# Router products of the residual as eight extra channels of the offset convolution, added behind PSUM, in a fused deformable-convolution, attention and mixture-of-experts kernel

## The chip, the cores and the metric

The kernel runs on one core of a Trainium2 chip, in one launch. The metric is the device time of that launch in microseconds. Everything is float32.

## The reference, cut to what matters

Four images of 256 channels and 64 x 64 pixels go through one layer of three parts. The change lies in the first part, and in a product that the third part needs.

```python
B, C, H, W = 4, 256, 64, 64
# 1: deformable 3x3 convolution of the group-normalized image, with a residual
n = groupnorm(x, groups=32)
om = conv3x3(n, w_off) + b_off            # 27 channels: 9 taps x (dy, dx), 9 masks
sampled[k] = bilinear(n, y + ky + dy[k], x + kx + dx[k]) * sigmoid(mask[k])
x = x + sum_k w_conv[:, :, k] @ sampled[k]
# 2: attention over the 4 images, on layer-normalized tokens
t = tokens(x)                             # 4 x 4096 tokens of 256
t = t + attention(layernorm(t))
# 3: mixture of 8 experts, each token to the best two
u = layernorm(t)
logits = u @ router_w.T                   # 8 columns
t = t + u + sum over the best two of gate_e * (gelu(u @ w1[e] + b1[e]) @ w2[e] + b2[e])
```

The router's product is linear up to the layer norm. So the kernel carries `t @ router_w.T`, eight columns, beside the 256 columns of `t` from the convolution on. A row of the convolution's output has `CR = 264` columns: 256 channels, and the eight products of those channels with the router's weights.

## The kernel before, in words

The first stage is the convolution, and it takes the first 2124 us. A prologue prepares image 0. Then come 1152 steps (`STEPS = 288` for each image): one step is one tap `k` of the nine for one tile `r` of 128 pixels. Nine steps make a tile, four tiles make a group of 512 pixels, whose output goes to DRAM in one store. The steps are written out by hand: within `tc.manual_schedule` the program order is each engine's order. For step `n`:

- `gather(n + 10)` and `gather(n + 11)`, for even `n`, are indirect DMAs that POOL issues (L577): for each of 128 pixels the four corners of the bilinear sample, 4 KB a pixel, from a `table` in DRAM, into one of ten buffers `g`. The first of the two waits for the last corner that reads the buffer.
- `corner0(n + 3)` on ACT (L593) starts the weighted sum `s` of the corners; `corners(n + 2)` on DVE (L601) adds the others, three operations a step, each with the gathered corner and `s` as inputs, both in SBUF.
- `turned(n)` on PE (L615) transposes `s` into PSUM, `to_sbuf(n)` on ACT (L621) copies it to `sT`.
- `product(n - 1)` on PE (L640) multiplies `sT` with the weights of the tap, 264 columns, and adds up in `acc`, a PSUM buffer for the tile. At the first tap of a tile it also adds the residual: two transposes of `xraw` (L628) give the 256 columns, and two products of `xraw` with the router's weights `rwc_sb` (L634) give the eight.
- `done`, once a tile, on ACT (L649): it copies the 264 columns of the tile that ended one step earlier from PSUM into `outs`, which has two buffers for groups of four tiles. After the fourth tile SP issues the store (L651).

In between, `pieces(b + 1)` prepares the next image, at due steps from step 32 on: group statistics on DVE (L302), the group norm's scale `rs` and shift `nb`, and from step 56 on eight `block`s, one every 22 steps. A block normalizes ten rows into `xs` on ACT (L362), transposes eight of them into the table (L369, L378, four stores on SP, L384), and runs the offset convolution: six PE products `po` of three taps by 32 channels, 96 rows (L396), three shifted copies of 32 rows each on ACT into `oc` (L408), four products with `tap_sum` that sum the three taps and transpose to pixels (L417), and a copy `kept` on DVE into `om` (L426). After the last block `positions` on DVE makes indices and weights. Image 3 has no next image, so there are no blocks beside its steps. Image 0's first three offset blocks and its whole table are made in the prologue, its other five offset blocks beside its own steps. In the prologue the tile framework orders the instructions, not the program by hand; its weights come by DMAs on SP, in the order `xraw`, `woff_sb` (L232), `boff_sb`, `wconv_sb` (L250), `rwc_sb`, and the router's columns of `wconv_sb` are made by `routed` at its end.

The two later stages, attention with the router's choice and the experts, read the stored rows and are not touched. In them L942 on DVE mixes the values of the images, with one input in PSUM and one in SBUF, L990 on DVE adds eight router columns in PSUM to such columns in SBUF, and L1105 is POOL's scatter of tokens.

Of the kernel before, what the change touches and what calls it, by code (L numbers as in the profile page):

```python
# [9 lines left out]
F32 = mybir.dt.float32  # L10
# [7 lines left out]
P = 128  # L18
# [52 lines left out]
def conv_attn_moe_kernel(  # L71
# [127 lines left out]
    with ExitStack() as actx:  # L199
# [26 lines left out]
        load_image(0)  # L226


        woff_sb = aw.tile([P, NCH, 3, 3, QUAD], F32, name="woff_sb")
        V.memset(woff_sb, 0.0)  # L230
        for ch in range(NCH):
            nc.sync.dma_start(  # L232
                woff_sb[:, ch, :, :, :NOFF],
                w_off[ch * P : (ch + 1) * P].rearrange("p (ki kj) o -> p ki kj o", kj=3),
            )
        boff_sb = aw.tile([3 * QUAD, 1], F32, name="boff_sb")
        V.memset(boff_sb, 0.0)
        nc.sync.dma_start(boff_sb[QUAD : QUAD + NOFF], b_off.unsqueeze(1))
        tap_sum = aw.tile([3 * QUAD, NOFF], F32, name="tap_sum")
        for kj in range(3):  # L240
            ps = slice(kj * QUAD, (kj + 1) * QUAD)
            V.tensor_copy(tap_sum[ps], ident[ps, kj * QUAD : kj * QUAD + NOFF])


        ocs = [aw.tile([3 * QUAD, RB, W], F32, name=f"oc{n}") for n in range(3)]
        for oc in ocs:
            V.memset(oc, 0.0)
        wconv_sb = aw.tile([P, NCH, K2, CR], F32, name="wconv_sb")
# [34 lines left out]


        params, stores = {}, {}

        def pieces(b):

# [8 lines left out]
            ve = asm.tile([P, NCH], F32, name=f"ve{b}", tag="gve", bufs=2)  # L297
            rs = asm.tile([P, NCH], F32, name=f"rs{b}", tag="grs", bufs=2)
            pm = []

            def stats(ch, j):
                V.bn_stats(st[:, ch, j, :], xr[:, ch, j * BLK : (j + 1) * BLK])  # L302
# [27 lines left out]
                (n + 5, lambda: G.tensor_tensor(rs, ve, nhalf[:, :NCH], ALU.pow))  # L330
            )
            out_.append((n + 7, shift))
            n += 8

            xrv = xr.rearrange("p ch (h w) -> p ch h w", w=W)
# [3 lines left out]
            def block(q, at, table=True, offsets=True, alone=False):  # L339

                out_ = [] if alone else later
                y0 = q * RB - 1
                lo, hi = max(y0, 0), min(y0 + RB + 2, H)
                t = {}
                between = "" if table else "_"

                def norm(ch):
                    if ch == 0:
                        t["xs"] = apad.tile(
                            [P, NCH, RB + 2, W], F32, name=f"xs{b}_{q}{between}",  # L350
                            tag=f"xs{between}", bufs=2 if table else 1,
                        )
                        if lo > y0:
                            G.memset(t["xs"][:, :, 0, :], 0.0)
                        if hi < y0 + RB + 2:
                            G.memset(t["xs"][:, :, RB + 1, :], 0.0)
                    to, of = t["xs"][:, ch, lo - y0 : hi - y0], xrv[:, ch, lo:hi]
                    scale, bias = rs[:, ch : ch + 1], nb[:, ch : ch + 1]
                    if alone:
                        V.tensor_scalar(to, of, scale, bias, ALU.mult, ALU.add)  # L360
                    else:
                        S.activation(to, of, AF.Identity, bias=bias, scale=scale)  # L362


                def turn(i):
                    xc = t["xs"][:, :, 1 : RB + 1].rearrange("p ch y x -> p ch (y x)")
                    t["tp"] = ps_tp.tile([P, C], F32, name=f"tpx{b}_{q}_{i}", tag="tp")
                    for ch in range(NCH):
                        T.transpose(  # L369
                            t["tp"][:, ch * P : (ch + 1) * P], xc[:, ch, i * P : (i + 1) * P],  # L370
                            ident,
                        )

                def leave(i):
                    if i == 0:
                        t["zt"] = ast.tile([P, NT, C], F32, name=f"zt{b}_{q}", tag="zt")
                    zt = t["zt"]
                    S.copy(zt[:, i, :], t["tp"])  # L378
                    if i < NT - 1:
                        return  # L380
                    for yl in range(2):
                        for two in range(2):
                            yy = q * RB + yl + 1 - two
                            stores[b] = nc.sync.dma_start(  # L384
                                tv[yy : yy + RB - 1 : 2, 1 : W + 1, two, :].rearrange(
                                    "t x c -> x t c"
                                ),
                                zt[yl * W : (yl + 1) * W],
                            )


                def rows_of(n):
                    if n == 0:
                        t["po"] = ps_om.tile([3 * QUAD, RB, W], F32, name=f"po{b}_{q}", tag="om")
                    ch, ki = divmod(n, 3)
                    T.matmul(  # L396
                        t["po"], woff_sb[:, ch, ki].rearrange("p kj o -> p (kj o)"),
                        t["xs"][:, ch, ki : ki + RB],
                        start=(n == 0), stop=(n == NCH * 3 - 1),
                    )  # L400

                oc = ocs[q % 2 if table else 2]

                def shifted(kj):
                    ps = slice(kj * QUAD, (kj + 1) * QUAD)
                    to = slice(max(0, 1 - kj), W - max(0, kj - 1))
                    of = slice(max(0, kj - 1), W - max(0, 1 - kj))
                    S.activation(  # L408
                        oc[ps, :, to], t["po"][ps, :, of], AF.Identity, bias=boff_sb[ps]
                    )  # L410

                def summed(half):
                    if half == 0:
                        t["pt"] = ps_om.tile([P, NT, NOFF], F32, name=f"pt{b}_{q}", tag="om")
                    ocf = oc.rearrange("p y x -> p (y x)")
                    for i in range(half * 2, half * 2 + 2):
                        T.matmul(  # L417
                            t["pt"][:, i, :], ocf[:, i * P : (i + 1) * P], tap_sum,
                            start=True, stop=True,
                        )  # L420

                def kept():
                    of[q] = om[:, rows_in(q), :] if b else atmp.tile(
                        [P, NT, NOFF], F32, name=f"om{b}_{q}", tag="om_", bufs=2
                    )
                    V.tensor_copy(of[q], t["pt"])  # L426

                out_.append((at, lambda: norm(0)))
                out_.append((at + 1, lambda: norm(1)))
                if table:  # L430
                    for i in range(NT):
                        out_.append((at + 3 + 4 * i, lambda i=i: turn(i)))
                        out_.append((at + 4 + 4 * i, lambda i=i: leave(i)))
                if offsets:
                    for m in range(NCH * 3):
                        out_.append((at + 4 + 2 * m + m // 2, lambda m=m: rows_of(m)))
                    for kj in range(3):
                        out_.append((at + 18 + kj, lambda kj=kj: shifted(kj)))
                    out_.append((at + 22, lambda: summed(0)))
                    out_.append((at + 23, lambda: summed(1)))  # L440
                    out_.append((at + 24, kept))
                return out_
# [180 lines left out]
        def product(n):  # L623
            b, r, k = split(n)
            if k == 0:
                accs[n // K2] = ps_acc.tile([P, BLK], F32, name=f"acc{b}_{r}", tag="acc")
                for ch in range(NCH):
                    T.matmul(  # L628
                        accs[n // K2][:, ch * P : (ch + 1) * P],
                        xraw[b][:, ch, r * P : (r + 1) * P], ident,  # L630
                        start=(ch == 0), stop=False, is_transpose=True,
                    )
                for ch in range(NCH):
                    T.matmul(  # L634
                        accs[n // K2][:, C:CR], xraw[b][:, ch, r * P : (r + 1) * P],
                        rwc_sb[:, ch, :], start=False, stop=False,
                    )
            sT = sTs.pop(n)
            for ch in range(NCH):
                T.matmul(  # L640
                    accs[n // K2][:, :CR], sT[:, ch * P : (ch + 1) * P], wconv_sb[:, ch, k, :],
                    start=False, stop=(k == K2 - 1 and ch == NCH - 1),
                )

        def done(tile_):
            b, r = divmod(tile_, NR)
            if r % NT == 0:
                outs[b] = ast.tile([P, NT, CR], F32, name=f"o{b}_{r}", tag="o")
            S.copy(outs[b][:, r % NT, :], accs.pop(tile_)[:, :CR])  # L649
            if r % NT == NT - 1:  # L650
                nc.sync.dma_start(t1[b][r // NT], outs[b])  # L651

# [902 lines left out]
```

## Time and profile before

| | |
|---|---|
| median of 14 runs | 3582.44 us (3573.46 to 3593.73) |
| profiled execution | 3575.61 us, span of its core 3573.8 us |
| mean granted TensorE clock | 0.929 of full speed |
| busy in the span: PE, DVE, POOL, ACT | 86%, 73%, 56%, 48% |
| HBM traffic | 899 MB, 252 GB/s over the span |
| first stage | steps from 90 us to 2124 us, about 1.77 us each |

In the profile a line names the source line, the engine, the operation and the tiles, output first, `out<-in`. PE is the matmul, PEld the load of the stationary operand, which overlaps it. A number in square brackets in the timeline is the engine's idle time ahead of the operation, with what ended it. The profiled execution is one run; its time stands beside the median in the table.

### The profile page before, as it was taken

How to read it: one execution, taken by the hardware profiler on the slowest of the kernel's cores; microseconds unless marked ns; L12 is line 12 of the kernel's file. 1: busy time of each engine (PE TensorE's matmuls, PEld its weight loads, DVE VectorE, ACT ScalarE, POOL GpSimd, SP SyncE). 2: the span in 40 equal slices, each digit the busy share in tenths (PEclk: the TensorE clock that was granted, in tenths of full speed). 3: DMA queues.
4: the chain of work that ended last, by engine and by line, in shares of the span. 5: the costliest groups of instructions: out<-in, count | busy, mean ns of one | idle time of the engine just before them, and what ended most of it. 6: DMA issues, size and time to landing. Idle time of an engine off the chain costs nothing. (4 is left out here: it accounts for less than half of the span.)

```text
span 3573.8 us, 49706 instructions
## 1 busy us (share of the span) xinstructions
PE 3059.5 (86%) x13658; PEld 2240.1 (63%) x13658; DVE 2605.5 (73%) x6747; ACT 1716.0 (48%) x3913; POOL 2004.8 (56%) x1801
## 2 busy tenths in 40 slices
PE   6799997889988899978777879997888888999995
PEld 4667765667766676756565654443444467888883
DVE  3777786867777777777676768887888864557777
ACT  2456653456544465644444434343333244555652
POOL 1565666766676666677776751110766656554441
PEclk7899998999999999999898889998999999999995
DMA  7899998899999899988788862112544344547778
GB/s 232 326 328 342 337 340 329 286 335 359 342 328 354 304 352 351 345 307 308 281 322 306 294 232 67 55 49 85 179 158 148 102 127 131 164 124 244 240 240 307
DMA packets 322442, 898.89 MB, mean 252 GB/s; under 512 B 43218, under 2 KB 89949, under 8 KB 320120
## 3 DMA queue, kind: packets, MB, share of 16 engines
q0 software_dynamic: 191808, 671.74, 51.8%
q1 hardware_dynamic: 130360, 223.98, 19.6%
q8 instruction: 113, 1.85, 0.2%
q14 instruction: 161, 1.32, 0.1%
HBM read 744.43 MB, written 154.79 MB: 252 GB/s over the span
## 5 line engine op out<-in xcount | busy, mean ns | idle before, releaser
L601 DVE SCALAR_TENSOR_TENSOR s<-g,wts,s 128x256 f32<-128x256 f32 x3456 | 1436.2, 481 | 519.3 <-ACT s L593 354.2
L577 POOL DMA_INDIRECT g<-table,idx x1152 | 1373.4, 1192 | 672.1 <-DVE s L601 393.6
L640 PE MATMUL acc<-wconv_sb,sT 128*128 128x264 f32 x4608 | 1334.7, 415 | 266.0 <-ACT sT L621 166.7
L640 PEld LDWEIGHTS acc<-wconv_sb,sT 128*128 128x128 f32 x4608 | 834.3, 202 | 409.0 <-ACT sT L621 196.0
L621 ACT COPY sT<-tps 128x256 f32<-128x256 f32 x1152 | 424.2, 368 | 736.0 <-PE tps L615 483.4
L593 ACT ACTIVATE s<-g,wts 128x256 f32<-128x256 f32 x1152 | 588.9, 511 | 234.7 <-DMA g<-table,idx 197.2
L615 PEld LDWEIGHTS tps<-ident,s 128*128 128x128 f32 x2304 | 329.1, 149 | 253.1 <-issue 161.6
L615 PE MATMUL tps<-ident,s 128*128 128x128 f32 x2304 | 461.8, 283 | 27.6 <-DVE s L601 23.4
L1379 POOL DMA_INDIRECT ys_rows<-y,to x284 | 282.0, 993 | 293.3 <-DVE y L1376 227.6
L1105 POOL DMA_INDIRECT xs_rows<-u,slots x256 | 259.9, 1015 | 126.9 <-issue 113.2
L1350 PE MATMUL ph<-xT,w 128*128 128x256 f32 x1136 | 276.8, 387 | 21.9 <-ACT hT L1354 11.9
L1368 PE MATMUL py<-w,hT 128*128 128x256 f32 x1136 | 272.8, 384 | 0.0
L1354 ACT ACTIVATE hT<-ph,w 128x256 f32<-128x256 f32 x284 | 133.3, 473 | 233.9 <-PE ph L1350 153.7
L1373 DVE TENSOR_TENSOR y<-py,w 128x512 f32<-128x512 f32 x142 | 98.3, 692 | 200.3 <-ACT w L1312 80.1
L1368 PEld LDWEIGHTS py<-w,hT 128*128 128x128 f32 x1136 | 219.5, 193 | 31.2
L1350 PEld LDWEIGHTS ph<-xT,w 128*128 128x128 f32 x1136 | 207.9, 193 | 48.9 <-ACT hT L1354 15.6
L173 POOL TENSOR_TENSOR l_rstd<-l_ve,nhalf 128x4 f32<-128x4 f32 x32 | 34.7, 1084 | 250.6 <-DVE l_ve L167 250.6
L396 PE MATMUL po<-xs,woff_sb 128*96 128x512 f32 x324 | 171.2, 614 | 0.0
L825 DVE SCALAR_TENSOR_TENSOR junk<-q,k 128x512 f32<-128x512 f32 x256 | 161.3, 690 | 8.6 <-ACT k L818 8.6
L947 ACT ACTIVATE gate<-pg,bg_c 128x512 f32<-128x512 f32 x64 | 43.3, 685 | 248.5 <-PE pg L748 195.0
L942 DVE SCALAR_TENSOR_TENSOR mix<-pv,att,mix 128x512 f32<-128x512 f32 x192 | 129.8, 744 | 3.6 <-PE pv L748 3.6
L974 PE MATMUL po<-wo_sb,mix 128*128 128x264 f32 x512 | 121.2, 391 | 8.1 <-DVE s L990 7.5
(245 smaller groups left out, 3360.9 us busy)
## 6 DMA issues: line engine op xcount, KB each, us to landing
xt<-xs_rows SPq DMA_DIRECT2D x142, 260.0 KB
table<-zt SPq DMA_DIRECT2D x128, 256.0 KB
early_state<-ys_rows SPq DMA_DIRECT2D x128, 256.0 KB
g<-table,idx POOLq DMA_INDIRECT x1152
t<-o SPq DMA_DIRECT2D x32, 528.0 KB
bt<-t SPq DMA_DIRECT2D x32, 528.0 KB
dt<-t SPq DMA_DIRECT2D x64, 264.0 KB
xraw<-in_x SPq DMA_DIRECT2D x16, 1024.0 KB
```

What stands on the lines that cost most here:

```text
L396: T.matmul(t["po"], woff_sb[:, ch, ki].rearrange("p kj o -> p (kj o)"), t["xs"][:, ch, ki : ki + RB], start=(n == 0), stop=(n == NCH * 3 - 1),
L577: g = G.indirect_dma_start(out=gs[n % NGB], out_offset=None, in_=tables[b], in_offset=bass.IndirectOffsetOnAxis(ap=params[b][0][:, r, k : ...
L593: first = S.activation(ss[n], gs[n % NGB][:, :C], AF.Copy, scale=params[b][1][:, 0, r, k : k + 1])
L601: last_corner[n] = V.scalar_tensor_tensor(ss[n], gs[n % NGB][:, c * C : (c + 1) * C], params[b][1][:, c, r, k : k + 1], ss[n], ALU.mult, A ...
L615: T.transpose(tps[n][:, ch * P : (ch + 1) * P], s[:, ch * P : (ch + 1) * P], ident)
L621: S.copy(sTs[n], tps.pop(n))
L640: T.matmul(accs[n // K2][:, :CR], sT[:, ch * P : (ch + 1) * P], wconv_sb[:, ch, k, :], start=False, stop=(k == K2 - 1 and ch == NCH - 1),)
L825: V.scalar_tensor_tensor(junk, qs[s_][:, ch, :], 1.0, ks[t_][:, ch, :], ALU.mult, ALU.mult, accum_out=parts[:, ch, s_ * B + t_, j : j + 1],)
L1105: s = G.indirect_dma_start(out=rows_, out_offset=bass.IndirectOffsetOnAxis(ap=slots[:, k, n : n + 1], axis=0), in_=u[:, n % NT, :], in_off ...
L1350: T.matmul(ph, w1_sb[:, ch, f * P : (f + 1) * P], xT[:, ch, :], start=(ch == 0), stop=(ch == NCH - 1),)
L1368: T.matmul(py[:, i, :], hT[:, f, i * P : (i + 1) * P], w2_sb[:, f, :], start=(f == 0), stop=(f == NCH - 1),)
L1379: s = G.indirect_dma_start(out=ys_rows[g], out_offset=bass.IndirectOffsetOnAxis(ap=to[:, i : i + 1], axis=0), in_=y[:, i, :], in_offset=No ...
```

## The change

The eight router columns of the residual are no longer made by two products per tile. The offset convolution gets eight more output channels, behind its 96: the middle tap's weights for them are the router's, divided by the group norm's scale (`router_of`, once an image, in one of two copies of the weights), so that the normalized rows give the products of the raw rows but for a constant per image. The constant is made by a product of the same weights with the shift `nb` (`shift_in`, `shift_out`) and taken off by a new activation `beside`, once a block, which copies the eight rows into `oc`. `tap_sum` has eight more columns that pass them through, and `kept` copies them into `routed_x`. `done` copies 256 columns on ACT and adds the eight columns of PSUM and of `routed_x` on DVE. The two transposes of `xraw` come behind the first tap's product instead of ahead of it. The weights `woff` come by six DMAs instead of two, `outs` has one buffer instead of two.

```diff
--- before.py
+++ after.py
@@ -226,23 +226,31 @@
         load_image(0)
 
 
-        woff_sb = aw.tile([P, NCH, 3, 3, QUAD], F32, name="woff_sb")
-        V.memset(woff_sb, 0.0)
+
+        TAPS = 3 * QUAD
+        OUTS = TAPS + NE
+        woffs = [aw.tile([P, NCH, 3, OUTS], F32, name=f"woff{n}") for n in range(2)]
+        for woff_sb in woffs:
+            V.memset(woff_sb, 0.0)
         for ch in range(NCH):
-            nc.sync.dma_start(
-                woff_sb[:, ch, :, :, :NOFF],
-                w_off[ch * P : (ch + 1) * P].rearrange("p (ki kj) o -> p ki kj o", kj=3),
-            )
-        boff_sb = aw.tile([3 * QUAD, 1], F32, name="boff_sb")
+            for ki in range(3):
+                nc.sync.dma_start(
+                    woffs[0][:, ch, ki, :TAPS].rearrange("p (kj o) -> p kj o", kj=3)[:, :, :NOFF],
+                    w_off[ch * P : (ch + 1) * P, ki * 3 : (ki + 1) * 3],
+                )
+        V.tensor_copy(woffs[1][:, :, :, :TAPS], woffs[0][:, :, :, :TAPS])
+        boff_sb = aw.tile([OUTS, 1], F32, name="boff_sb")
         V.memset(boff_sb, 0.0)
         nc.sync.dma_start(boff_sb[QUAD : QUAD + NOFF], b_off.unsqueeze(1))
-        tap_sum = aw.tile([3 * QUAD, NOFF], F32, name="tap_sum")
+        tap_sum = aw.tile([OUTS, NOFF + NE], F32, name="tap_sum")
+        V.memset(tap_sum, 0.0)
         for kj in range(3):
             ps = slice(kj * QUAD, (kj + 1) * QUAD)
-            V.tensor_copy(tap_sum[ps], ident[ps, kj * QUAD : kj * QUAD + NOFF])
-
-
-        ocs = [aw.tile([3 * QUAD, RB, W], F32, name=f"oc{n}") for n in range(3)]
+            V.tensor_copy(tap_sum[ps, :NOFF], ident[ps, kj * QUAD : kj * QUAD + NOFF])
+        V.tensor_copy(tap_sum[TAPS:OUTS, NOFF:], ident[TAPS:OUTS, TAPS:OUTS])
+
+
+        ocs = [aw.tile([OUTS, RB, W], F32, name=f"oc{n}") for n in range(3)]
         for oc in ocs:
             V.memset(oc, 0.0)
         wconv_sb = aw.tile([P, NCH, K2, CR], F32, name="wconv_sb")
@@ -283,6 +291,7 @@
 
 
         params, stores = {}, {}
+        routed_x = {}
 
         def pieces(b):
 
@@ -297,6 +306,9 @@
             ve = asm.tile([P, NCH], F32, name=f"ve{b}", tag="gve", bufs=2)
             rs = asm.tile([P, NCH], F32, name=f"rs{b}", tag="grs", bufs=2)
             pm = []
+            woff_sb = woffs[b % 2]
+            shift_of = asm.tile([OUTS, 1], F32, name=f"shift{b}", tag="shift", bufs=2)
+            routed_x[b] = ap_.tile([P, NR, NE], F32, name=f"rx{b}", tag="rx")
 
             def stats(ch, j):
                 V.bn_stats(st[:, ch, j, :], xr[:, ch, j * BLK : (j + 1) * BLK])
@@ -330,6 +342,30 @@
                 (n + 5, lambda: G.tensor_tensor(rs, ve, nhalf[:, :NCH], ALU.pow))
             )
             out_.append((n + 7, shift))
+
+            def router_of():
+
+                V.tensor_tensor(ve, ve, rs, ALU.mult)
+                for ch in range(NCH):
+                    V.tensor_scalar(
+                        woff_sb[:, ch, 1, TAPS:], rwc_sb[:, ch, :], ve[:, ch : ch + 1], None,
+                        ALU.mult,
+                    )
+
+            def shift_in():
+                pm.append(ps_om.tile([OUTS, 1], F32, name=f"ps{b}", tag="om"))
+                for ch in range(NCH):
+                    T.matmul(
+                        pm[-1], woff_sb[:, ch, 1], nb[:, ch : ch + 1],
+                        start=(ch == 0), stop=(ch == NCH - 1),
+                    )
+
+            def shift_out():
+                V.tensor_scalar(shift_of[TAPS:], pm[-1][TAPS:], -1.0, None, ALU.mult)
+
+            out_.append((n + 8, router_of))
+            out_.append((n + 9, shift_in))
+            out_.append((n + 10, shift_out))
             n += 8
 
             xrv = xr.rearrange("p ch (h w) -> p ch h w", w=W)
@@ -391,11 +427,10 @@
 
                 def rows_of(n):
                     if n == 0:
-                        t["po"] = ps_om.tile([3 * QUAD, RB, W], F32, name=f"po{b}_{q}", tag="om")
+                        t["po"] = ps_om.tile([OUTS, RB, W], F32, name=f"po{b}_{q}", tag="om")
                     ch, ki = divmod(n, 3)
                     T.matmul(
-                        t["po"], woff_sb[:, ch, ki].rearrange("p kj o -> p (kj o)"),
-                        t["xs"][:, ch, ki : ki + RB],
+                        t["po"], woff_sb[:, ch, ki], t["xs"][:, ch, ki : ki + RB],
                         start=(n == 0), stop=(n == NCH * 3 - 1),
                     )
 
@@ -409,9 +444,14 @@
                         oc[ps, :, to], t["po"][ps, :, of], AF.Identity, bias=boff_sb[ps]
                     )
 
+                def beside():
+                    S.activation(
+                        oc[TAPS:], t["po"][TAPS:], AF.Identity, bias=shift_of[TAPS:]
+                    )
+
                 def summed(half):
                     if half == 0:
-                        t["pt"] = ps_om.tile([P, NT, NOFF], F32, name=f"pt{b}_{q}", tag="om")
+                        t["pt"] = ps_om.tile([P, NT, NOFF + NE], F32, name=f"pt{b}_{q}", tag="om")
                     ocf = oc.rearrange("p y x -> p (y x)")
                     for i in range(half * 2, half * 2 + 2):
                         T.matmul(
@@ -423,7 +463,8 @@
                     of[q] = om[:, rows_in(q), :] if b else atmp.tile(
                         [P, NT, NOFF], F32, name=f"om{b}_{q}", tag="om_", bufs=2
                     )
-                    V.tensor_copy(of[q], t["pt"])
+                    V.tensor_copy(of[q], t["pt"][:, :, :NOFF])
+                    V.tensor_copy(routed_x[b][:, rows_in(q), :], t["pt"][:, :, NOFF:])
 
                 out_.append((at, lambda: norm(0)))
                 out_.append((at + 1, lambda: norm(1)))
@@ -436,6 +477,7 @@
                         out_.append((at + 4 + 2 * m + m // 2, lambda m=m: rows_of(m)))
                     for kj in range(3):
                         out_.append((at + 18 + kj, lambda kj=kj: shifted(kj)))
+                    out_.append((at + 21, beside))
                     out_.append((at + 22, lambda: summed(0)))
                     out_.append((at + 23, lambda: summed(1)))
                     out_.append((at + 24, kept))
@@ -624,29 +666,26 @@
             b, r, k = split(n)
             if k == 0:
                 accs[n // K2] = ps_acc.tile([P, BLK], F32, name=f"acc{b}_{r}", tag="acc")
+            sT, acc = sTs.pop(n), accs[n // K2]
+            for ch in range(NCH):
+                T.matmul(
+                    acc[:, :CR], sT[:, ch * P : (ch + 1) * P], wconv_sb[:, ch, k, :],
+                    start=(k == 0 and ch == 0), stop=(k == K2 - 1 and ch == NCH - 1),
+                )
+            if k == 0:
                 for ch in range(NCH):
                     T.matmul(
-                        accs[n // K2][:, ch * P : (ch + 1) * P],
-                        xraw[b][:, ch, r * P : (r + 1) * P], ident,
-                        start=(ch == 0), stop=False, is_transpose=True,
-                    )
-                for ch in range(NCH):
-                    T.matmul(
-                        accs[n // K2][:, C:CR], xraw[b][:, ch, r * P : (r + 1) * P],
-                        rwc_sb[:, ch, :], start=False, stop=False,
-                    )
-            sT = sTs.pop(n)
-            for ch in range(NCH):
-                T.matmul(
-                    accs[n // K2][:, :CR], sT[:, ch * P : (ch + 1) * P], wconv_sb[:, ch, k, :],
-                    start=False, stop=(k == K2 - 1 and ch == NCH - 1),
-                )
+                        acc[:, ch * P : (ch + 1) * P], xraw[b][:, ch, r * P : (r + 1) * P],
+                        ident, start=False, stop=False, is_transpose=True,
+                    )
 
         def done(tile_):
             b, r = divmod(tile_, NR)
             if r % NT == 0:
-                outs[b] = ast.tile([P, NT, CR], F32, name=f"o{b}_{r}", tag="o")
-            S.copy(outs[b][:, r % NT, :], accs.pop(tile_)[:, :CR])
+                outs[b] = ast.tile([P, NT, CR], F32, name=f"o{b}_{r}", tag="o", bufs=1)
+            acc = accs.pop(tile_)
+            S.copy(outs[b][:, r % NT, :C], acc[:, :C])
+            V.tensor_tensor(outs[b][:, r % NT, C:], acc[:, C:CR], routed_x[b][:, r], ALU.add)
             if r % NT == NT - 1:
                 nc.sync.dma_start(t1[b][r // NT], outs[b])
```

## The prediction

> **What bounds the kernel now.** Everything the change touches lies in the first stage, the deformable convolution, from 0 to 2124 us of a 3573.8 us span. The page comes first. It makes TensorE look like the bound:
>
> ```profile
> PE 3059.5 (86%) x13658; PEld 2240.1 (63%) x13658; DVE 2605.5 (73%) x6747; ACT 1716.0 (48%) x3913; POOL 2004.8 (56%) x1801
> ```
>
> Second, the windows by stretch. I cut each image's 288 steps by the starts of L593 into the part in which the blocks of the offset convolution run beside them (steps 56 to 235) and the rest. Image 3 has no blocks beside it, as no image follows.
>
> ```profile
> 188.20:347.50 159.30, 154.78 (x768) 113.91 (x767) 119.82 (x316) 100.50 (x243) 102.03 (x95) 1.00 0.94 334
> 859.20:1011.10 151.90, 140.85 (x705) 107.10 (x703) 110.97 (x270) 89.54 (x226) 99.21 (x91) 0.97 0.95 350
> 1699.80:1860.50 160.70, 124.11 (x597) 97.54 (x596) 111.31 (x269) 72.71 (x191) 112.30 (x94) 0.89 0.85 308
> 1860.50:2022.70 162.20, 128.19 (x605) 102.21 (x603) 111.08 (x270) 72.20 (x189) 117.25 (x88) 0.86 0.81 290
> ```
>
> After the length the columns are PE, PEld, DVE, ACT, POOL, clock, DMA share. The second and the fourth row are 89 steps each: 1.71 us a step with PE 93% busy, and 1.82 us with PE 79% busy. A stretch with less PE work is the slower one. So two different limits hold: with blocks PE (92 to 97% busy), without them something that is no engine's busy time. Third, the timeline of POOL and DVE alone shows it:
>
> ```profile
> 531.83 1.25 POOL L577 DMA_INDIRECT g<-table,idx  x1 [0.30 <-DVE s L601]
> 533.38 9.20 POOL L577 DMA_INDIRECT g<-table,idx  x1 [0.30 <-issue]
> 542.88 0.94 POOL L577 DMA_INDIRECT g<-table,idx  x1 [0.30 <-issue]
> ...
> 532.17 9.59 DVE L601 SCALAR_TENSOR_TENSOR s<-g,wts,s 128x256 f32<-128x256 f32 x24
> 546.36 1.27 DVE L601 SCALAR_TENSOR_TENSOR s<-g,wts,s 128x256 f32<-128x256 f32 x3 [4.60 <-ACT s L593]
> ```
>
> A gather's issue takes 0.94 us, but this one 9.20 us: it ends 0.8 us after DVE's 24 corners without a gap (both inputs in SBUF) end, and then DVE has no data for 4.6 us. The trace has 24 such issues of over 3.3 us in this stage, with DVE busy through 95% of them; all issues together take 286 us more than at 0.94 us. Fourth, what lets POOL in:
>
> ```profile
> 503.64 2.06 POOL L577 DMA_INDIRECT g<-table,idx  x1 [0.30 <-issue]
> ...
> 501.25 3.65 DVE L601 SCALAR_TENSOR_TENSOR s<-g,wts,s 128x256 f32<-128x256 f32 x9 [0.35 <-issue]
> 504.82 0.26 DVE L426 COPY om<-pt 128x108 f32<-128x108 f32 x1
> 505.00 1.27 DVE L601 SCALAR_TENSOR_TENSOR s<-g,wts,s 128x256 f32<-128x256 f32 x3
> ```
>
> DVE does not stop here either, but one of its operations reads PSUM; the issue ends 0.88 us after that operation begins. No issue of over 2.1 us has a copy from PSUM in it. In the later stage, 35 scatters of POOL lie beside L942 alone (one input in PSUM, one in SBUF), with a median of 0.96 us and none over 1.07.
>
> **The change, part by part.** (A) *The add.* `done` gets a DVE add of 8 columns, one input in PSUM, one in SBUF, after the corners of every ninth step. It is of the kind that lets POOL in. I counted in the trace: 26 long issues contain the place of an add at least 1 us before their end. Each add lets one issue through; the next one stands behind the same run of corners again. So an add is worth one issue and its gap, 0.94 + 0.30 = 1.24 us, and 26 of them 32 us; it need not become time, as after a run the data may also be late by its own way. Ends: 0, and 60 us if all blocked time behind the first add went. I take three quarters, 24 us off, near to the 32, since DVE starves after these runs (4.6 us above).
>
> The add waits for the product of the step before last. At 302.60 us, where one would stand, that product had ended at 301.32 us; where PE lags, DVE's next corners stand behind the add, then POOL's gathers that wait for them, but PE still has two transposes and two products of its own before it needs them. Cost of the wait: 0.
>
> The Trainium skill, page "SBUF — State Buffer", section "SBUF: two separate sides", has the shared port held by a two-input DVE operation for that instruction alone; by that rule POOL would come in after 0.4 us at every corner, and term A would be 0. The 9.20 us issue above speaks against that reading, and I go by the row.
>
> (B) *PE loses the router's products*, four loads and matmuls per tile:
>
> ```profile
> 426.18 0.25 PEld L628 LDWEIGHTS acc<-ident,xraw 128*128 128x128 f32 x2
> 426.39 0.53 PEld L634 LDWEIGHTS acc<-rwc_sb,xraw 128*128 128x128 f32 x4
> 426.84 0.75 PEld L640 LDWEIGHTS acc<-wconv_sb,sT 128*128 128x128 f32 x4
> ```
>
> From 426.39 to 426.84, 0.45 us a tile, 58 us for 128 tiles. Without blocks (68 tiles) PE waits anyway: 0. With blocks (537 steps, 60 tiles) 27 us at most. In image 0 (20 tiles, 97% busy) I count all, 9 us; in images 1 and 2 (40 tiles, 92% busy, where gathers also hold) half, 9 us: 18 us off. Ends: 58 us off, and a loss of 16 us, which is the second rival. The two transposes that go behind the product are moved, not added; what they covered is the wait for `sT`, which in the stretch from 188 to 501 us cost PE 6 us in all even so: nothing. Eight more columns of weights (104 instead of 96) in 0.17 us loads and eight more columns in `pt`: under 1 us.
>
> (C) *ACT gets `beside`*, 32 times, three of them in the prologue. Row L408 has 0.672 us for the same 512 columns; it goes by columns, not by partitions. It stands in the one step of a block's last six that had no extra ACT work: three steps of 0.88 + 0.67 and two of 0.88 + 0.92 us lie around it. 29 x 0.67 = 19 us, half of it on the path, as PE's summed products and data already landed cover the rest: 10 us. Ends 0 and 19.
>
> (D) *DVE*: 128 adds at 0.165 us (row L990, PSUM and SBUF, 16 columns) and 32 second copies at 0.15 to 0.27 us: 28 us of work, on an engine that idles 519 us before L601. 4 us on the path; ends 0 and 28.
>
> (E) *One buffer for `outs`.* ACT's copy and DVE's add of the next tile now wait until the store has landed; behind them stand the next `corner0`, `sT` and corners. By the DMA packets, 28 of the 31 stores land at least 5 us before the next group's first copy; the others at 3.6 us after it (242.3 against 238.8 us; four table stores were ahead on SP), 1.7 and 0.8 us before it. With about 1 us from the last packet to the wait's end: 4 us. Ends 0 and 10.
>
> (F) *The prologue.* Four more DMAs of weights on SP, ahead of `wconv_sb`, `rwc_sb` and the first tables: the packets are the same 2304 (7.37 us of issue), plus 4 x 0.33 us (L651's issue) = 1.3 us. `rwc_sb` was needed at 70 us; now `router_of` needs it, three DVE operations of 0.16 us, ahead of PE's `shift_in` (four loads) and the first offset products. It landed at 22.2 us, so now 23.5, and block 0's first transpose stood at 22.4 us: 0 to 2.5 us, by how the prologue is ordered. With three `beside` on ACT (2 us), which holds the chain at 48 to 52 us: 3 us. Ends 0 and 5. Per later image, three small DVE operations, four PE loads and a copy: under 1 us each, beside the steps. The extra memsets and the copy of the weights lie under the image's load.
>
> Sum: -24 - 18 + 10 + 4 + 4 + 3 = -21 us. The profiled execution took 3575.61 us (2 us around its span), so it would be 3555. It is 7 us below the median of the 14 runs, 3582.44; the forecast is for the median: **3561 us**.
>
> **The rivals.** *No change.* The issue let in by an add is followed by one that is blocked just as long, and the starving ends no sooner: A is 0. For it: an add brings one issue, not the end of a run. Against it: DVE waited 72 us for L593 in image 3's middle. -21 + 24 = +3, 3585 us.
>
> *Slower: the clock.* Place: the stretches with blocks. Less PE work lets the granted clock fall: 1.00, 0.97, then 0.89 and 0.86 in the four rows above, with PE 97, 93, 77 and 79% busy. In image 3's steps 56 to 235 a step takes 1.80 us against 1.735 with blocks, 0.07 us for 14 points of PE. The change takes 0.45/9 = 0.05 us a step, 2.9 points: 0.014 us x 1152 = 16 us, in place of 18 us off: +13 us, 3595 us. It decides if the clock from 188 to 1510 us falls by 0.02 or more. Against it: part of image 3's loss is blocked POOL, which A mends.
>
> The Trainium skill, page "TensorE: Matmul & The Clock Gate", section "HAM oscillation — how this bites in real kernels", says that gaps in PE's work make the clock drop; it speaks against the change, and by it alone the time is the second rival's.
>
> *A larger gain.* All blocked time behind the adds goes (60), B is 27, and `beside` is covered: -87 + 11 = -76 us, 3506 us.
>
> **How the numbers follow.** A measurement of this kernel can tell about 0.2% (7 us) from no change. The forecast (3545 to 3575 by its own ends) has 0.45, no change 0.18, the clock 0.20, the larger gain 0.10; 0.07 is left for C, E and F at their upper ends with A at 0: 3582 - 18 + 19 + 4 + 10 + 5 = 3602. Faster 0.53, same 0.17, slower 0.30. The range reaches into the larger gain and past the slower cases: 3525 to 3602.
>
> **What would show it.** A right: issues of L577 over 3.3 us fall from 24 to about 15, and an issue ends some 0.9 us after an add; wrong: they last as before. B right: steps 56 to 235 of image 0 fall from 1.75 to about 1.70 us with the clock at 1.00. C: PE's idle time before L640 by `sT` grows with blocks. E: ACT's `o` copy waits for a DMA near 240 us. F: the first gather comes up to 5 us after 78.6 us. If the gain lies outside the first stage, or steps 235 to 288 of the images (1.80 to 1.91 us a step) do not gain, the reasons are wrong.

## The result, and the profile after

The changed kernel takes 3646.12 us (median of 10 runs, 3615.54 to 3675.56), the kernel before 3586.76 us beside it (47 runs): the ratio is 1.0158, 95% interval 1.0134 to 1.0182. One of the ten runs, 3675.56 us, fell in a slower state of the chip; the ratio leaves it out, and without it the median is 3644.70 us, 58 us above the kernel before. The forecast was 3561 us, its range ended at 3602. The profiled execution has a span of 3642.8 us at a mean granted clock of 0.917, against 3573.8 us and 0.929.

The first line of the page has PE relieved by only 8 us, and 10 us more work on DVE and 33 us more on ACT:

```profile
PE 3051.8 (84%) x13162; PEld 2194.3 (60%) x13162; DVE 2615.1 (72%) x6927; ACT 1748.8 (48%) x3945; POOL 2054.0 (56%) x1801
```

The windows by stretch, cut at the same steps as before (length, PE, PEld, DVE, ACT, POOL, clock, DMA share, GB/s). The first row, with blocks and PE 97% busy, is 1.9 us shorter than its counterpart; the second, also with blocks, is 6.5 us longer. The two rows of image 3, with no block beside them, are 7.1 and 6.7 us longer at a lower clock:

```profile
187.00:344.40 157.40, 152.81 (x731) 109.67 (x730) 120.14 (x335) 105.09 (x247) 106.87 (x95) 1.00 0.95 339
870.50:1028.90 158.40, 140.34 (x666) 105.13 (x665) 112.25 (x286) 94.54 (x230) 104.80 (x91) 0.94 0.94 340
1745.60:1913.40 167.80, 124.56 (x556) 94.36 (x555) 112.29 (x282) 73.34 (x191) 116.22 (x93) 0.86 0.83 298
1913.40:2082.30 168.90, 125.72 (x557) 96.00 (x556) 108.49 (x273) 72.41 (x189) 114.45 (x87) 0.83 0.78 280
```

From one image's first `corner0` to the next image's (for image 3, to its own last one), the four images take 512.6, 511.4, 518.6 and 552.8 us, before 510.8, 505.5, 500.3 and 511.0. Of the 68 us more, 42 lie in image 3, which has no offset convolution beside it: the new channels, `beside` and the prologue can't be what costs most. What image 3 does have is the add. These are the page's groups of DVE in the steps, first the corners of the kernel before, then the corners and the add of the changed kernel. Behind the first bar stand busy time and mean ns, behind the second the idle time ahead of the group and what ended most of it:

```profile
L601 DVE SCALAR_TENSOR_TENSOR s<-g,wts,s 128x256 f32<-128x256 f32 x3456 | 1436.2, 481 | 519.3 <-ACT s L593 354.2
```

```profile
L643 DVE SCALAR_TENSOR_TENSOR s<-g,wts,s 128x256 f32<-128x256 f32 x3456 | 1428.2, 481 | 372.3 <-ACT s L635 245.8
L688 DVE TENSOR_TENSOR o<-acc,rx 128x8 f32<-128x8 f32 x128 | 21.4, 167 | 202.3 <-ACT o L687 170.4
```

The add works 21.4 us, and DVE stands 202.3 us in front of it. Before, DVE idled 519.3 us ahead of the corners; now it is 372.3 + 202.3 = 574.6 us, 55 us more. What the add waits for, by the answer for its line (us in all, times):

```profile
its engine sat idle before it (us, times) until:
  ACT o L687: 170.4, 82
  ACT sT L663: 18.2, 13
  issue: 7.9, 7
  ACT s L635: 5.8, 6
```

Not PE, whose product the prediction looked at, but ACT: the copy `o` of the other 256 columns of the same PSUM tile `acc`. The copy stands on ACT behind `corner0` and `sT`. The timeline of image 3 shows one turn of it:

```profile
1955.62 10.77 DVE L643 SCALAR_TENSOR_TENSOR s<-g,wts,s 128x256 f32<-128x256 f32 x27
...
1958.02 9.20 POOL L619 DMA_INDIRECT g<-table,idx  x1 [0.30 <-issue]
...
1970.51 0.51 ACT L635 ACTIVATE s<-g,wts 128x256 f32<-128x256 f32 x1 [5.57 <-DMA g<-table,idx]
1970.93 0.35 ACT L663 COPY sT<-tps 128x256 f32<-128x256 f32 x1
1971.18 0.38 ACT L687 COPY o<-acc 128x256 f32<-128x256 f32 x1
...
1971.59 0.17 DVE L688 TENSOR_TENSOR o<-acc,rx 128x8 f32<-128x8 f32 x1 [5.20 <-ACT o L687]
1971.67 1.27 DVE L643 SCALAR_TENSOR_TENSOR s<-g,wts,s 128x256 f32<-128x256 f32 x3
```

DVE's run of 27 corners holds a gather's issue for 9.20 us; the gathered data is then late, and ACT's `corner0(n + 3)` waits 5.57 us for it. Most of the add's 5.20 us is this wait, and DVE would have had it anyway: the corner behind the add needs the `s` that this `corner0` writes (that is why the idle time ahead of the corners fell from 519.3 to 372.3 us). But `s` is there at 1971.02 us, and without the add the corners could start. With it they start at 1971.67 us, as ACT first does `sT(n)` and the copy, and the add comes after the copy: some 0.6 us. The 58 us more of the median are 0.45 us for each of the 128 tiles. Issues of over 8 us, which the add was to cut short, are 15 against 8 before: where it has to wait, as here, it stands at the head of DVE's next run, not inside one.

### The profile page after: what moved, and what is told of

The parts are those of the page before. It is cut to its first block, busy times and chain, and to the rows that moved or that the text cites. A ratio compares the mean times of both kernels' runs of the same rounds, so it can differ in the third digit from the quotient of the medians.

```text
span 3642.8 us, 48931 instructions
## 1 busy us (share of the span) xinstructions
PE 3051.8 (84%) x13162; PEld 2194.3 (60%) x13162; DVE 2615.1 (72%) x6927; ACT 1748.8 (48%) x3945; POOL 2054.0 (56%) x1801
## 5 line engine op out<-in xcount | busy, mean ns | idle before, releaser
L619 POOL DMA_INDIRECT g<-table,idx x1152 | 1421.1, 1234 | 690.3 <-DVE s L643 405.7
L643 DVE SCALAR_TENSOR_TENSOR s<-g,wts,s 128x256 f32<-128x256 f32 x3456 | 1428.2, 481 | 372.3 <-ACT s L635 245.8
L671 PE MATMUL acc<-wconv_sb,sT 128*128 128x264 f32 x4608 | 1357.2, 421 | 322.4 <-ACT sT L663 188.5
L671 PEld LDWEIGHTS acc<-wconv_sb,sT 128*128 128x128 f32 x4608 | 852.4, 206 | 471.6 <-ACT sT L663 219.8
L657 PE MATMUL tps<-ident,s 128*128 128x128 f32 x2304 | 473.8, 289 | 46.8 <-DVE s L643 41.2
L657 PEld LDWEIGHTS tps<-ident,s 128*128 128x128 f32 x2304 | 318.6, 151 | 290.8 <-issue 221.4
L688 DVE TENSOR_TENSOR o<-acc,rx 128x8 f32<-128x8 f32 x128 | 21.4, 167 | 202.3 <-ACT o L687 170.4
L432 PE MATMUL po<-xs,woff 128*104 128x512 f32 x324 | 165.2, 597 | 0.0
```

The source lines that it names most:

```text
L432: T.matmul(t["po"], woff_sb[:, ch, ki], t["xs"][:, ch, ki : ki + RB], start=(n == 0), stop=(n == NCH * 3 - 1),)
L619: g = G.indirect_dma_start(out=gs[n % NGB], out_offset=None, in_=tables[b], in_offset=bass.IndirectOffsetOnAxis(ap=params[b][0][:, r, k : ...
L643: last_corner[n] = V.scalar_tensor_tensor(ss[n], gs[n % NGB][:, c * C : (c + 1) * C], params[b][1][:, c, r, k : k + 1], ss[n], ALU.mult, A ...
L657: T.transpose(tps[n][:, ch * P : (ch + 1) * P], s[:, ch * P : (ch + 1) * P], ident)
L671: T.matmul(acc[:, :CR], sT[:, ch * P : (ch + 1) * P], wconv_sb[:, ch, k, :], start=(k == 0 and ch == 0), stop=(k == K2 - 1 and ch == NCH - 1),
```

## The experiments

Theory: the add pauses DVE, because it is held behind ACT's copy of the same PSUM tile. Rivals: the missing work of PE (a lower clock, or other effects), the offset convolution's additions, the single buffer of `outs`. The runs were made on four chips: on one, the kernel before takes 3586 us, on three others, called quick below, 3264 to 3267 us, so each ratio is against the kernel before on the same chip.

**The order of the two readers turned round** (3586 us chip):

```diff
-            S.copy(outs[b][:, r % NT, :C], acc[:, :C])
             V.tensor_tensor(outs[b][:, r % NT, C:], acc[:, C:CR], routed_x[b][:, r], ALU.add)
+            S.copy(outs[b][:, r % NT, :C], acc[:, :C])
```

> The changed kernel with one pair of lines in done swapped: DVE's add ahead of ACT's copy, so that the add waits for the product alone and ACT's copy waits for the add. The pause (theory 1: the add waits for ACT's copy, which stands behind corner0 and sT, and DVE stands still for 1.6 us a tile): the idle time ahead of the add falls from 202 us to under 40, image 3's steps from 1.91 to about 1.80 us, the time from 3646 to 3590 or less. The clock (theory 2: PE lost work, and the granted clock fell from 0.929 to 0.917): 3646 within 10 us, clock at 0.917.

Measured: 3573.17 us, ratio 0.9962 (0.9932 to 0.9992). Two lines swapped give back 72 us. The answer for the add's line, and the corners' group:

```profile
its engine sat idle before it (us, times) until:
  remote: 25.3, 6
  PE tps L657: 15.5, 8
  PE acc L671: 9.8, 15
  issue: 3.8, 6
  DMA t<-o: 3.7, 2
```

```profile
L643 DVE SCALAR_TENSOR_TENSOR s<-g,wts,s 128x256 f32<-128x256 f32 x3456 | 1436.7, 482 | 452.5 <-ACT s L635 302.6
```

No wait for ACT's copy is left (`remote` is a wait whose end the profile can't name); the idle time ahead of the add is 58 us in place of 202, though under 40 were expected, and that of DVE in the steps 452.5 + 58 = 510 us, 9 below the kernel before. The granted clock is 0.919, hardly above the 0.917 of the changed kernel and below the 0.929 of the kernel before, and yet this version is faster than both: the clock isn't what made the changed kernel slow. Image 3 alone (524.1 us) stays above the 511.0 of before.

**The pause alone, in the kernel before** (3586 us chip). All else as before; the result of the added operation goes to a tile of its own, not to `outs`:

```diff
-            S.copy(outs[b][:, r % NT, :], accs.pop(tile_)[:, :CR])
+            acc = accs.pop(tile_)
+            S.copy(outs[b][:, r % NT, :], acc[:, :CR])
+            V.tensor_tensor(spare8, acc[:, C:CR], eight, ALU.add)
```

> The kernel before, with a DVE add of eight columns of acc into a spare tile behind ACT's copy, once a tile; nothing else of the change. The pause: the add waits for ACT's copy as in the changed kernel, 150 to 200 us in all, and the time rises from 3587 by 35 to 60 us. The clock: PE's work is the same, so 3587 to 3595.

Measured: 3625.57 us, ratio 1.0129 (1.0087 to 1.0171). One operation of 0.167 us a tile, whose result nobody uses, costs 39 us by the medians, and 46 us by the ratio. The answer for its line:

```profile
its engine sat idle before it (us, times) until:
  ACT o L653: 165.7, 83
  issue: 15.7, 11
  ACT sT L624: 14.8, 12
```

That is the changed kernel's wait again, 165.7 us in 83 places against 170.4 in 82. As the operation doesn't write `outs`, the two engines meet in `acc` alone: two reads of one PSUM tile are kept in the order in which the program has them. Image 3 takes 541.5 us.

**The same operation ahead of the copy,** called the break below (3586 us chip), with the `S.copy` and the `V.tensor_tensor` of the last diff in the other order:

> The kernel before, with the same DVE add ahead of ACT's copy, so that it waits for the product alone. The pause: no wait of note, 3580 to 3595. The prediction's term A (an operation that reads PSUM lets one gather issue through): 3560 to 3570, and fewer issues of over 3.3 us. The clock: 3587.

Measured: 3578.43 us, ratio 0.9973 (0.9949 to 0.9997). This is part A of the prediction by itself, and it lies between the two expectations: just below the 3580 to 3595 without a gain, and short of the 3560 to 3570 of part A. The timelines of POOL and of DVE:

```profile
1960.81 6.82 POOL L580 DMA_INDIRECT g<-table,idx  x1 [0.30 <-issue]
1967.93 2.15 POOL L580 DMA_INDIRECT g<-table,idx  x1 [0.31 <-DVE s L604]
```

```profile
1958.40 8.40 DVE L604 SCALAR_TENSOR_TENSOR s<-g,wts,s 128x256 f32<-128x256 f32 x21 [0.22 <-ACT s L596]
1966.72 0.16 DVE L653 TENSOR_TENSOR spare<-acc,eight 128x8 f32<-128x8 f32 x1
1966.79 2.46 DVE L604 SCALAR_TENSOR_TENSOR s<-g,wts,s 128x256 f32<-128x256 f32 x6
```

The issue ends at 1967.63 us, 0.91 us after the operation that reads PSUM begins, though DVE never stops. Eight of the 12 issues over 5 us end so, 0.90 to 0.91 us after it. No issue over 8 us is left (8 before), but 27 over 3.3 us (24 before), and the time of all issues beyond 0.94 us fell only from 291 to 284 us (over all 1152 issues; the prediction has 286 for the first).

**PE's part alone** (3586 us chip): `product` as in the changed kernel, nothing else.

```diff
-                for ch in range(NCH):
-                    T.matmul(
-                        accs[n // K2][:, C:CR], xraw[b][:, ch, r * P : (r + 1) * P],
-                        rwc_sb[:, ch, :], start=False, stop=False,
-                    )
...
```

> The kernel before, with the changed kernel's product: without the two router products of the residual (that part of the output is left out), the two transposes behind the first tap's product. No add, no extra channels. The pause: PE has less to do and nobody waits, 3565 to 3590. The clock: 3625 to 3645, with the clock at 0.92 or less.

Measured: 3599.30 us, ratio 1.0041 (1.0016 to 1.0067): less work of PE, and 13 us more, outside both expected ranges. The clock and the corners' group of its profile:

```profile
core 0: 3604.9 us, clock 0.914
```

```profile
L601 DVE SCALAR_TENSOR_TENSOR s<-g,wts,s 128x256 f32<-128x256 f32 x3456 | 1433.6, 481 | 540.8 <-ACT s L593 360.2
```

Clock and blocked issues both went the wrong way: 0.914 for 0.929 in the profiled runs (0.917 for 0.925 in the mean of all), and 18 issues over 8 us for 8. Image 3 has most of the loss, 532.2 us. The other chips come next. First the order of PE's products, with nothing left out:

```diff
+            sT, acc = sTs.pop(n), accs[n // K2]
+            for ch in range(NCH):
+                T.matmul(
+                    acc[:, :CR], sT[:, ch * P : (ch + 1) * P], wconv_sb[:, ch, k, :],
...
+            if k == 0:
...
-                        accs[n // K2][:, C:CR], xraw[b][:, ch, r * P : (r + 1) * P],
+                        acc[:, C:CR], xraw[b][:, ch, r * P : (r + 1) * P],
                         rwc_sb[:, ch, :], start=False, stop=False,
```

> The kernel before with its two router products kept, and those and the two transposes put behind the first tap's product. PE's work is that of before, the order that of the changed kernel. pe_side cost 13 us, with 18 gather issues of over 8 us where before has 8, and the granted clock at 0.914. If the missing work is the cause (clock, or PE that no longer slows DVE's runs): 3580 to 3590, clock at 0.93, some 8 issues of over 8 us. If the order is the cause (nothing covers the wait for sT at a tile's start): 3595 to 3605.

Measured: 3266.76 us against 3267.12, ratio 0.9997 (0.9984 to 1.0009). The order costs nothing on this chip. The expectation was written for the 3586 us chip, and on that one the order alone was not run.

**The changed kernel without the add**, on the same chip: ACT copies all 264 columns.

```diff
-            S.copy(outs[b][:, r % NT, :C], acc[:, :C])
-            V.tensor_tensor(outs[b][:, r % NT, C:], acc[:, C:CR], routed_x[b][:, r], ALU.add)
+            S.copy(outs[b][:, r % NT, :], acc[:, :CR])
```

> The changed kernel without the add: ACT copies all 264 columns (the residual's router products, though made by the convolution, are left out of the output). The pause: without DVE's wait 3585 to 3605, which is pe_side's 3599 and what the extra channels and the one buffer cost or bring. If the extra channels on ACT (beside) and the one buffer are the cost: 3630 or more.

Measured: 3249.44 us, ratio 0.9953 (0.9938 to 0.9967). Everything of the change but the add is a gain of 18 us here, where the expectation, again for the 3586 us chip, had a small loss or none.

**The add taken late, once a group of four tiles, between two SBUF tiles**, two steps behind the last copy and just ahead of the store:

```diff
+        def group_done(tile_):
...
+            V.tensor_tensor(outs[b][:, :, C:], outs[b][:, :, C:], routed_x[b][:, rows], ALU.add)
+            nc.sync.dma_start(t1[b][r // NT], outs[b])
```

> The changed kernel with ACT copying all 264 columns, and one DVE add of 4 x 8 columns in SBUF per group of four tiles, two steps later, ahead of the store: 32 adds instead of 128, none of them reading PSUM. The pause: the copy is long done, so no wait, and 3585 to 3605 as in no_add. If the add's operand in PSUM is what helps (term A, before_break): 5 to 15 us behind add_first's 3573. If only the number of waits counts: 3595 to 3605, a quarter of the pause's 57 us over 3587.

Measured: 3283.41 us, ratio 1.0050 (1.0030 to 1.0070). The store comes later, and there is one buffer: ACT's copy waits for it (us in all, times).

```profile
  DMA t<-o: 28.7, 6
```

Without the add this wait is 10.7 us in 3 places, so 18 of the 25 us between the spans of the two profiled runs are this wait. A late add moves the cost, it doesn't save it.

**One buffer for `outs`, in the kernel before:**

```diff
-                outs[b] = ast.tile([P, NT, CR], F32, name=f"o{b}_{r}", tag="o")
+                outs[b] = ast.tile([P, NT, CR], F32, name=f"o{b}_{r}", tag="o", bufs=1)
```

> The kernel before with one buffer for outs instead of two. The prediction's term E: 4 us, 3587 to 3596. If the waits for the store are a cause of the loss: 3600 or more, with ACT waiting for a DMA ahead of its copy.

Measured: 3271.61 us, ratio 1.0020 (1.0008 to 1.0032). ACT's copy waits as the prediction had it, in three places:

```profile
  DMA t<-o: 10.0, 3
```

**The main runs again on a quick chip,** beside a kernel before of 3264.35 us. The changed kernel:

> The changed kernel as it is, beside its variants on one chip (two chips differed: the kernel before took 3586 us on one and 3267 us on the other, where gather issues of over 3.3 us were 8 instead of 24). If the loss needs the long blocked issues: 1.016 where before takes some 3590 us, under 1.005 where it takes some 3270 us. If the pause costs by itself, as DVE is the bound of the quick chip too (1.34 us a step in image 3, three corners of 0.40 us and a gap): 1.01 or more on both.

Measured: 3313.43 us, ratio 1.0156 (1.0135 to 1.0176). The loss is there on a quick chip too, and so are the add's waits for ACT's copy:

```profile
  ACT o L687: 114.2, 111
```

With the add ahead of the copy:

> The changed kernel with the add ahead of ACT's copy. The pause: 0.990 to 0.998 of before on either chip, and 30 to 75 us below the changed kernel beside it. On the quick chip less of the gain comes from the long issues, as there are few, so the lower end of the gain there.

Measured: 3257.81 us, ratio 0.9983 (0.9974 to 0.9993); the swap gives back 56 us here. The ratio is just above the 0.990 to 0.998 expected. Without the add:

> The changed kernel without the add (that part of the output is left out). It was 0.995 of before on the quick chip. There it should be so again; on the slow chip the prediction's term A is missing, so 1.000 to 1.005, behind add_first_again by some 15 us, as pe_side (1.004) lost there.

Measured: 3249.62 us, ratio 0.9961 (0.9946 to 0.9977). So an add ahead of the copy still costs some 8 us (the two intervals overlap a little), of the 64 that it costs behind it. Last, the add ahead of the copy, and the store of two tiles at a time from two half buffers, in the same space as the one buffer:

```diff
-                nc.sync.dma_start(t1[b][r // NT], outs[b])
+                nc.sync.dma_start(t1[b][r // NT][:, i : i + 2], outs[b])
```

> add_first with stores of two tiles from two buffers of two tiles, in the same memory as one of four: 64 stores instead of 32, and ACT waits for none. one_buffer cost 0.2% with 10 us of waits for the store. Term E undone: 5 to 10 us below add_first_again. If the wait for the store was covered here, or the smaller stores cost as much: the same within 3 us.

Measured: 3253.65 us, ratio 0.9964 (0.9952 to 0.9976). On this chip the version beats both kernels, the kernel before by 11 us and the changed one by 60. It is 4 us below the version with one buffer, where 5 to 10 were expected or none; that is the size of the one buffer's price, though the two intervals touch.

**What was open: PE's part on a quick chip,** beside a kernel before of 3264.92 us. The edit alone, then with the operation on PSUM of the break, then the order alone:

> The kernel before with TensorE's products of the residual and the router's weights left out (the eight router columns lack the residual's part) and the two transposes behind the first product. Theory 'clock': less TensorE work lowers the granted clock and the time rises, ratio 1.003 to 1.006 with a clock 0.01 to 0.02 below that of the kernel before. Theory 'blocked gathers': ratio 1.003 to 1.006 where gathers are slow, at most 1.000 where they are quick (kernel before at about 3265 us), with the issues of over 8 us more numerous than in the kernel before.

> The same, and once a tile an operation of DVE that reads eight columns of PSUM, ahead of ACT's copy of the tile and with its result unused. Theory 'blocked gathers': the operation lets POOL in, the issues of over 8 us go, and the loss with them: ratio 0.995 to 1.000. Theory 'clock': the clock stays down and the ratio is that of the kernel without the operation less 0.003 at most, 1.001 to 1.004.

> The kernel before with the residual's two transposes and the router's four products behind the first tap's product instead of ahead of it; nothing is left out. Both theories: 0.999 to 1.001; a ratio over 1.002 would put the loss on the order and clear the missing products.

Measured: 3249.52 us, ratio 0.9948 (0.9931 to 0.9966), clock 0.957; with the operation 3244.28 us, 0.9940 (0.9922 to 0.9957), and issues over 8 us fall from 3 to none; the order alone 3262.90 us, 0.9998 (0.9985 to 1.0011), clock 0.957. Less work of PE is a gain of 15 us here, at the same clock. The 13 us lost on the other chip are therefore no general price of it. Whether the clock, the blocked gathers or the order made them there stays open: the order and the break were tried only on quick chips, where there was no loss to mend, and the intervals with and without the break overlap. And the pause, again:

> The kernel before with an operation of DVE on eight columns of the tile in PSUM behind ACT's copy of it, its result unused. The pause has the same price on every chip: 1.012 to 1.017. If the price depends on slow gathers, it is 1.010 to 1.015 where the kernel before takes 3587 us and under 1.008 where it takes 3265 us.

Measured: 3308.78 us, ratio 1.0143 (1.0124 to 1.0161), 44 us. The pause has about the same price on a chip with slow gathers and on one with quick ones, so the first of its two expectations held.

## Why the prediction was wrong

**The step that failed** is the second half of part A, "The add waits for the product of the step before last. ... Cost of the wait: 0." It asked when PE would be ready and named what is queued behind the add on DVE, but it did not ask who else touches `acc`. ACT's copy stands one line above the add in `done`, reads the same tile, and is placed in ACT's order behind `corner0(n + 3)` and `sT(n)`. The first corner behind the add needs `corner0(n + 3)` alone; with the add it needs `sT(n)` and the copy too. In place of 0 the step is 39 to 44 us by the medians in the kernel before (0.31 to 0.34 us a tile), and 56 to 72 us in the changed one, against the same kernel with the two lines swapped (0.43 to 0.56 us a tile; the copy by itself takes 0.38 us). Why the changed kernel pays more was not tried. With that number in it the sum would have been on the right side. None of the rivals had it: the slower rival was another mechanism.

**A, the gain:** right in kind, too large in size. The issue does end 0.9 us after the operation. But the forecast was 24 us, and the break alone gave 8 us (by its interval 1 to 18). The step that was mis-sized is "an add is worth one issue and its gap": blocked time fell by 7 us, not by 32, as the next issue stands behind the same run. That was the argument of the rival "no change", and it was the better one. In the changed kernel itself not even that came, as an add that waits falls between two runs: blocked time rose to 338 us. On the rule weighed there, the Trainium skill, page "SBUF — State Buffer", section "SBUF: two separate sides", has the shared port locked for the whole of one instruction. Here POOL's issue took 6.82 us beside a run of 21 corners of DVE, and the next operation with PSUM in it let it in, so the row was the right guide for the mechanism.

**B, PE's relief:** 18 us off were forecast. Alone it gave 15 us off on a quick chip and 13 us more on the 3586 us chip, where the forecast was made. In the changed kernel, image 0's steps 56 to 235 took 1.73 us in place of 1.75 (1.70 were forecast), at the clock 1.00. The rival of the clock gave a loss of 16 us, near the 13, but had its place in the stretches with blocks; the loss of that run lies mostly in image 3, where PE is least busy. The Trainium skill, page "TensorE: Matmul & The Clock Gate", section "HAM oscillation — how this bites in real kernels", has the clock drop where PE is idle for more than some 3.4 us. In the traces' steps PE has 24 such gaps between matmuls in the kernel before and 34 in PE's part alone on the 3586 us chip, with the clock at 0.929 and 0.914. On a quick chip PE's part alone has 3, and so has the order alone, both at 0.957. That agrees with the page, but the kernel with the swapped lines has 23 at 0.919, and a blocked gather leaves such gaps too; what comes first is not shown.

**C, D, E, F:** together 21 us in the sum. On the quick chips PE's part alone (0.9948) and all of the change but the add (0.9953 and 0.9961) differ by 2 to 4 us, with intervals of some 5 us to either side: that is what there is for C, E, F and DVE's second copies. C's 10 us were not seen there. F is none: the first `corner0` starts at 90.0 us, before at 90.3. E, 4 us, measured 4.5 and 4.2 us; in the changed kernel its copy has no wait for a store. D's 4 us are some 8 for the add, when it is not held.

The prediction's own signs did tell it: issues over 3.3 us went from 24 to 30, not to 15, and the loss is greatest where there are no blocks.

## What to carry to other kernels

When two engines are to read one PSUM tile, the order of the two lines in the program was a wait between the engines here, though neither writes it (165.7 us in 83 of 128 tiles); put the engine that sets the pace first, and the one with slack behind it. Before a new operation's wait is priced at nothing, list every instruction that touches its operands, reads included, and see what stands ahead of each on its own queue. A short operation's cost is what its engine would have done meanwhile: here 0.17 us of work cost 0.3 to 0.6 us a tile.

## What was not expected of the hardware

The same program takes 3586 us on one chip and 3264 to 3267 us on three others. In image 3 the median 4 KB packet of a gather takes 159 ns in the kernel before on the slow one and 159 to 161 ns in kernels run on the quick ones (the mean 181 against 164 to 170 ns); but from the first packet to the last a gather takes a median of 1.9 us on the slow one and 1.44 us on the quick ones, and image 3 takes 511 us against some 384. Why the packets come further apart was not tried.

A run of corners without a gap holds POOL's issue for as long as the run lasts, up to 9.20 us, and one operation of 0.16 us that has an input in PSUM freed it in 0.91 us. The issue behind it is held again, so the cut is worth much less than the stretch that it takes off the one issue.
